# A vision tower's tokenizer: two linear layers folded into one product of 512 columns

## The chip, the core and the metric

The kernel runs on one core of one Trainium2 chip. The time is that of one execution on the device, in microseconds; the figure of the kernel before is the median of three runs. A core has a matrix engine (TensorE, PE in the profile, whose weight loads are listed as PEld), three more compute engines (VectorE or DVE, ScalarE or ACT, GpSimd or POOL) and SyncE (SP), which only issues transfers. Each engine works through its own queue of instructions in order; semaphores between them say when operands are ready. Products of TensorE go to PSUM, in which this kernel rotates seven tiles of 128 x 512 float32, called banks below.

## The reference

A tower of two transformer layers over four images of 3 x 224 x 224 in float32. Only the tokenizer is touched by the change. An image is cut into 28 x 28 patches of 8 x 8 x 3 = 192 numbers, 3136 tokens in all:

```python
tokens = layernorm(patches, ln1_g, ln1_b)
tokens = tokens @ W1 + b1                     # 192 -> 256
tokens = layernorm(tokens, ln2_g, ln2_b)
q = tokens
k = tokens
tokens = jnp.concatenate([q, k, tokens], axis=1)
h1 = layernorm(tokens @ Wp1 + bp1, lnp_g, lnp_b)   # 256 -> 256
h1 = jax.nn.silu(h1)
return h1 @ Wp2 + bp2                         # 256 -> 256
```

`layernorm` subtracts the mean over the features, multiplies by rsqrt(variance + 1e-5), then applies g and b. The concatenation makes three copies of each image's tokens, one after another; the shape of the later layers follows from it, but the kernel computes each token once. After the tokenizer come a layer with an attention across the images and routed experts (the token products with Wk, Wv and so on), and a layer with another attention and gated experts.

## The kernel before

**Tiles and groups.** Tokens are worked in 28 tiles of 112 (one tile is four rows of patches of one image, TT = 112), four tiles make a group (GT = 4), so there are seven groups. D = 256 is held in two chunks of 128 partitions where a token runs along the free axis, and 112 partitions where tokens are the partitions.

**Loads.** The image tile `img` holds one row of patches per partition (4 x 28 = 112), 24 rows of pixels (three colours by eight lines) and eight rows of zeros. It comes in four transfers, two on SP's and two on ScalarE's queue (L211). Behind them on SP are W1 (L219), Wp1, Wp2, the attention's weights, and then the zero fill of the two row buffers `xrows` and `yrows` that the experts use later (L253, 38 transfers of 1 MB). Behind them on ScalarE are the two rows of ln1. POOL's queue issues fifteen small constant loads (L170), then b1, bp1, bp2, bo (through `spread`, L184) and rb2, and then sets `nothing`, the source of the zero fill, to zero (L249). The norm rows ln2 and lnp are among the fifteen; one transposition (L446) makes columns of them.

**Patches.** A `manual_schedule` block (L430 to L448) fixes the order on TensorE and VectorE as written; elsewhere the tile scheduler decides it, and both engines keep their queue's order. For k = 0 to 6, `turn_patches(k)` (L338) turns four columns of patches: a half c takes 16 products with the identity (L347), each of which gives 32 rows for 112 patch rows. The rows lie in the 32-partition strip g, columns j of a half differ in their place along the free axis. ScalarE copies each half to `pT` (L352). Float32 products take two passes and are two records each. The order inside a half is

```python
for j in range(GT):
    for g in range(4):
        nc.tensor.matmul(pt[32 * g : 32 * (g + 1), j * TT : (j + 1) * TT], ...)
```

VectorE takes the statistics of the same pixels, one BN_STATS per column (L443). Ahead of k = 5 stands `first_layer()` (L356 to L395): it multiplies W1 by ln1_g, subtracts from each column its mean over the inputs (so the patch's own mean needs no subtraction), adds ln1_b W1 to b1, and permutes the rows of W1 to the order of `pT` (L390). After the last column `patch_scales` (L398 to L419) makes the reciprocals of all 3136 standard deviations (112 x 28) in one go and brings them to tokens as `rtok`.

**The loop.** `tokenize(g)` (L499 to L528) is a pipeline over three groups. In one call TensorE transposes the normalised rows of the second layer (group g-1) and of the third (group g-2), eight transposes each (L297), and then takes 16 passes for each of the three linear layers (L317): first layer of group g, second of g-1, third of g-2. ScalarE leaves the transposed rows with the norm's g and b applied (L492: Identity for ln2, Silu for lnp), and takes a square root per layer and group (L474). VectorE scales the first product by `rtok` and adds b1 (L466), or adds the bias of the later layers (L461), takes statistics and their aggregate per tile (L470, L471), the reciprocal (L479) and the normalised rows (L482). Calls 7 and 8, which finish the last groups, stand inside the first layer's attention (L1042, L1044), where the order of TensorE, VectorE and ScalarE is written out: `tokenize(7)`, keys and values of group 0, `tokenize(8)`, keys and values of group 1 and so on. Each of these starts with eight transposes of normalised tokens (L297).

## Time and profile before

| what | value |
|---|---|
| median of three runs | 854.3 us (852.16 to 854.61) |
| the profiled execution | 813.35 us |
| its span, first to last instruction | 811.6 us |
| mean granted TensorE clock | 0.973 |
| TensorE busy | 735.7 us, 91% |
| weight loads | 519.4 us, 64% |
| VectorE, ScalarE, POOL busy | 514.5, 318.5, 132.5 us |
| first turned patch on TensorE | 17.75 us |
| first product of the first layer | 40.18 us |
| start of the loop's passes (transposes) | 72.55, 85.06, 97.57, 110.09 us |
| transposes of the attention's groups 0 and 1 | 137.09, 151.17 us |

The profile is of one execution, which was shorter than the runs of the median; its durations and gaps belong together, and its own total is the 813.35. A line of the timeline gives start, duration, engine, source line, operation with its result and operands, the number of instructions gathered in it, and in brackets the idle time ahead of it with what ended it. A line of the windows gives, for a stretch of time, the busy time and number of instructions of PE, PEld, DVE, ACT and POOL, then the granted TensorE clock, the mean busy share of the 16 DMA engines and the rate in GB/s. In the slices of the span each digit is the busy share of a fortieth of the span (20.3 us) in tenths.

### The profile page before, as it was taken

The page shows a single profiled execution, that of the slowest core. Times are in us where ns is not written, and L with a number is a line of the kernel's source. Part 1 is how long each engine was busy: PE and PEld are TensorE (multiplying, and loading weights), DVE is VectorE, ACT ScalarE, POOL GpSimd, SP SyncE. Part 2 cuts the span into 40 slices and gives each one's busy share as a digit, 9 for nine tenths or more (in the row PEclk, how much of TensorE's full clock was granted, in tenths as well). Part 3 has the DMA queues.
Part 4 walks back from the last instruction along what each step waited for, and adds up shares of the span by engine and source line. Part 5 has one row for each costly group of instructions (what it writes and reads, how often), then busy time and mean ns, then how long its engine had stood idle before and what let it go on. Part 6 is the DMA issues. An engine that isn't in the chain of part 4 may idle for free. (4 is left out here: it accounts for less than half of the span.)

```text
span 811.6 us, 11184 instructions
## 1 busy us (share of the span) xinstructions
PE 735.7 (91%) x3669; PEld 519.4 (64%) x3669; DVE 514.5 (63%) x1619; ACT 318.5 (39%) x758; POOL 132.5 (16%) x151
## 2 busy tenths in 40 slices
PE   1879998899798887999999999799999999999996
PEld 1757785555455555887888887375776675555553
DVE  3477887576668886436445756699985655554431
ACT  0414443545375475443222322627544503222221
POOL 4200000000006360760012030775000000000000
PEclk9999999999999988999999999899999999999999
DMA  8999992000001168443334234232000002333323
GB/s 182 343 426 422 420 421 85 1 0 1 0 1 56 36 207 260 137 139 104 94 101 137 92 107 131 85 86 69 1 1 1 0 20 69 88 98 93 94 85 113
DMA packets 59182, 97.52 MB, mean 120 GB/s; under 512 B 15486, under 2 KB 49460, under 8 KB 54260
## 3 DMA queue, kind: packets, MB, share of 16 engines
q1 hardware_dynamic: 52700, 81.47, 29.1%
q0 software_dynamic: 6224, 14.13, 6.1%
q10 hardware_dynamic: 200, 1.21, 0.7%
q8 instruction: 29, 0.48, 0.2%
q14 instruction: 29, 0.24, 0.1%
HBM read 31.04 MB, written 65.74 MB: 119 GB/s over the span
## 5 line engine op out<-in xcount | busy, mean ns | idle before, releaser
L901 POOL DMA_INDIRECT xrows<-xn,pos x56 | 60.2, 1074 | 274.2 <-ACT kq L665 233.4
L1369 POOL DMA_INDIRECT ys<-yrows,pos x56 | 57.0, 1018 | 142.1 <-DMA yrows<-yb 126.0
L1173 PE MATMUL pb<-xTb,own 128*128 128x256 f32 x240 | 58.8, 389 | 3.8 <-DVE r L764 1.6
L1173 PE MATMUL pb<-hb,own 128*128 128x256 f32 x240 | 57.1, 380 | 0.3 <-DVE hb L1181 0.3
L1190 PE MATMUL pyb<-own,hb 128*128 128x256 f32 x240 | 57.0, 380 | 0.2 <-ACT hb L1179 0.2
L1179 ACT ACTIVATE hb<-pb,own 128x256 f32<-128x256 f32 x74 | 35.0, 473 | 55.9 <-PE pb L1173 47.5
L297 PE MATMUL pt<-ident,xn 112*128 112x112 f32 x280 | 42.2, 282 | 12.6 <-DVE xn L482 6.9
L1173 PEld LDWEIGHTS pb<-xTb,own 128*128 128x128 f32 x240 | 44.6, 194 | 12.5 <-ACT hb L1179 1.9
L1574 PE MATMUL pqk<-Wqkv,lxT 128*112 128x512 f32 x112 | 49.7, 594 | 0.5 <-ACT lxT L81 0.5
L1190 PEld LDWEIGHTS pyb<-own,hb 128*128 128x128 f32 x240 | 45.4, 190 | 6.7 <-ACT hb L1179 0.6
L297 PEld LDWEIGHTS pt<-ident,xn 112*128 112x128 f32 x280 | 32.4, 148 | 26.6 <-ACT xn L778 9.6
L1173 PEld LDWEIGHTS pb<-hb,own 128*128 128x128 f32 x240 | 43.3, 190 | 5.9 <-DVE hb L1181 0.9
L1196 DVE TENSOR_TENSOR yb<-pyb,eb 128x512 f32<-128x512 f32 x30 | 20.7, 690 | 39.2 <-PE pyb L1190 38.8
L306 PE MATMUL pe<-xT,eW 128*128 128x448 f32 x112 | 45.2, 546 | 0.0
L1163 ACT COPY xTb<-ptb 128x512 f32<-128x512 f32 x30 | 17.5, 583 | 64.3 <-PE ptb L1159 64.3
L1181 DVE TENSOR_SCALAR hb<-pb,own 128x256 f32<-128x256 f32 x46 | 22.1, 481 | 29.5 <-PE pb L1173 29.5
L317 PE MATMUL pwo<-Wo,oT 128*112 128x256 f32 x112 | 29.0, 413 | 7.5 <-DVE oT L730 6.7
L1574 PEld LDWEIGHTS pqk<-Wqkv,lxT 128*112 128x112 f32 x112 | 19.3, 177 | 24.8 <-issue 22.7
L690 DVE SCALAR_TENSOR_TENSOR prod<-kq 128x784 f32<-128x784 f32 x32 | 30.3, 968 | 7.3 <-ACT kq L665 5.1
L1582 ACT ACTIVATE qk<-qk 112x256 f32<-112x256 f32 x56 | 22.8, 407 | 27.9 <-DVE qk L1578 25.4
L306 PEld LDWEIGHTS pe<-xT,eW 128*128 128x128 f32 x112 | 20.2, 190 | 20.9 <-issue 20.7
L1150 DVE COPY own<-ew 128x1540 f32 x30 | 28.9, 963 | 5.0 <-issue 1.5
(339 smaller groups left out, 1520.1 us busy)
## 6 DMA issues: line engine op xcount, KB each, us to landing
xrows<-nothing SPq DMA_DIRECT2D x19, 1024.0 KB
yrows<-nothing SPq DMA_DIRECT2D x19, 1024.0 KB
out_dram<-h SPq DMA_DIRECT2D x84, 112.0 KB
xb<-xrows SPq DMA_DIRECT2D x30, 256.0 KB
yrows<-yb SPq DMA_DIRECT2D x30, 256.0 KB
ew<-in_L_ffn_expert_w_dram SPq DMA_DIRECT2D x6, 768.0 KB
wb<-wd SPq DMA_DIRECT2D x28, 112.0 KB
img<-in_x_dram ACTq DMA_DIRECT2D x2, 588.0 KB
```

What stands on the lines that cost most here:

```text
L297: nc.tensor.transpose(pt[:, j * TT : (j + 1) * TT], xn[:, j, c * P : (c + 1) * P], ident[:TT, :TT])
L306: nc.tensor.matmul(pm[: wcols.stop - wcols.start, :n], w[:, c, wcols], xT(c), start=(c == 0), stop=(c == chunks - 1),)
L317: nc.tensor.matmul(pm[:, i, :], xT(c, t), w[:, c, :], start=(c == 0), stop=(c == chunks - 1))
L690: nc.vector.scalar_tensor_tensor(prod, qTs[s][:, o, :], 1.0, kT[:, o, t * SEQ : (t + 1) * SEQ], ALU.mult, ALU.mult, accum_out=atts[s][:, o ...
L901: put = nc.gpsimd.indirect_dma_start(out=xrows[:, :], out_offset=bass.IndirectOffsetOnAxis(ap=pos[:, k, t0 + j : t0 + j + 1], axis=0), in_ ...
L1150: nc.vector.tensor_copy(w, ewf[0][:, bass.ds(off, EW)])
L1173: nc.tensor.matmul(pm, wm[:, c, o * P : (o + 1) * P], src[:, c, :], start=(c == 0), stop=(c == 1),)
L1179: nc.scalar.activation(dst[:, o, :], pm, AF.Relu, bias=b)
L1190: nc.tensor.matmul(pm[:, t, :], src[:, c, t * P : (t + 1) * P], wm[:, c, :], start=(c == 0), stop=(c == 1),)
L1369: got = nc.gpsimd.indirect_dma_start(out=y[:, j, k, :], out_offset=None, in_=yrows[:, :], in_offset=bass.IndirectOffsetOnAxis(ap=pos[:, k, ...
L1574: nc.tensor.matmul(pqk, xT[:, c, cut(j, 1)], Wqkv[:, c, : 2 * D], start=(c == 0), stop=(c == 1),)
L1582: nc.scalar.activation(half, half, AF.Square, accum_out=ss[:, j, i : i + 1])
```

## The change

Because W1 has had its column means taken out, a token after the first layer is p/s with p = x W1c + s b1', where x are the raw pixels, s is the patch's standard deviation (the root of variance + eps) and b1' = b1 + ln1_b W1. The second norm of p/s is (p - mean p) / sqrt(var p + eps s²), so s only enters under the root. The second layer is linear in that, so its weights are folded in: `Wall` holds, side by side, W1c with the row b1' (256 columns, of which only the variance of p is used) and that matrix times W2 (256 columns), where W2 is ln2_g Wp1 with its column means taken out. The std is written into the image tile's zero row 24, one number per patch, and is turned with the pixels; it meets b1' in the product.

So `first_layers` (once, ahead of all patches) makes `Wall`; `patch_stds(k)` makes the standard deviations of four columns ahead of their `turn_patches(k)`; in `turn_patches` the strip g is now the outer and the column j the inner loop; `scaled_variances` brings eps s² to tokens as `ev`; `first_rows(g)` takes the product of 512 columns, one tile to a PSUM bank, of which ScalarE copies the right half and VectorE takes the statistics of the left, and then makes the rows of the third layer. The rows between the first and the second layer are no longer normalised or transposed. The second layer's product, its `y2`, and the Identity with ln2 are gone. Loads of ln1, ln2, W1 and Wp1 now stand ahead of the image on ScalarE's and SP's queues, and b1 and bp1 are issued next on POOL's. The diff, cut:

```diff
-    allones = const.tile([TT, TT], F32, tag="allones", name="allones")
+    allones = const.tile([P, P], F32, tag="allones", name="allones")
...
-        ("ln2_g", "L0_tok_ln2_g"), ("ln2_b", "L0_tok_ln2_b"), ("lnp_g", "L0_tok_lnp_g"),
-        ("lnp_b", "L0_tok_lnp_b"), ("gamma", "L0_attn_gamma"), ("beta", "L0_attn_beta"),
+        ("lnp_g", "L0_tok_lnp_g"), ("lnp_b", "L0_tok_lnp_b"), ("gamma", "L0_attn_gamma"), ("beta", "L0_attn_beta"),
...
     img = tokp.tile([TT, 32, WID], F32, tag="img", name="img")
+    ln1 = tokp.tile([2, PD], F32, tag="ln1", name="ln1")
+    nc.scalar.dma_start(out=ln1[:1], in_=a["L0_tok_ln1_g"].unsqueeze(0))
+    nc.scalar.dma_start(out=ln1[1:], in_=a["L0_tok_ln1_b"].unsqueeze(0))
+    ln2 = tokp.tile([4, P], F32, tag="ln2", name="ln2")
+    nc.scalar.dma_start(out=ln2[:2], in_=a["L0_tok_ln2_g"].rearrange("(r p) -> r p", p=P))
+    nc.scalar.dma_start(out=ln2[2:], in_=a["L0_tok_ln2_b"].rearrange("(r p) -> r p", p=P))
+    W1 = tokp.tile([KP, 2, D], F32, tag="W1", name="W1")
+    nc.sync.dma_start(out=W1, in_=a["L0_tok_W1"].rearrange("(s p) n -> p s n", p=KP))
+    Wp1 = tokp.tile([P, 2, D], F32, tag="Wp1", name="Wp1")
+    nc.sync.dma_start(out=Wp1, in_=a["L0_tok_Wp1"].rearrange("(c p) n -> p c n", p=P))
     for b in range(NI):
 ...
-    ln1 = tokp.tile([2, PD], F32, tag="ln1", name="ln1")
-    nc.scalar.dma_start(out=ln1[:1], in_=a["L0_tok_ln1_g"].unsqueeze(0))
-    nc.scalar.dma_start(out=ln1[1:], in_=a["L0_tok_ln1_b"].unsqueeze(0))
-    W1 = tokp.tile([KP, 2, D], F32, tag="W1", name="W1")
-    nc.sync.dma_start(out=W1, in_=a["L0_tok_W1"].rearrange("(s p) n -> p s n", p=KP))
+    b1 = spread(tokp, "b1", a["L0_tok_b1"])
+    bp1 = spread(tokp, "bp1", a["L0_tok_bp1"])
     nc.vector.memset(img[:, CY:, :], 0.0)
...
-    b1 = spread(tokp, "b1", a["L0_tok_b1"])
-    Wp1 = tokw.tile([P, 2, D], F32, tag="Wp1", name="Wp1", bufs=1)
-    nc.sync.dma_start(out=Wp1, in_=a["L0_tok_Wp1"].rearrange("(c p) n -> p c n", p=P))
-    bp1 = tokw.tile([TT, D], F32, tag="bp1", name="bp1", bufs=1)
-    nc.gpsimd.dma_start(out=bp1, in_=a["L0_tok_bp1"].partition_broadcast(TT))
     Wp2 = tokw.tile([P, 2, D], F32, tag="Wp2", name="Wp2", bufs=1)
     nc.sync.dma_start(out=Wp2, in_=a["L0_tok_Wp2"].rearrange("(c p) n -> p c n", p=P))
...
+    SROW = 3 * 32 + CY
     def turn_patches(k):
         for c in range(2):
             pt = ps_tile("ptp")
-            for j in range(GT):
-                for g in range(4):
+            for g in range(4):
+                for j in range(GT):
                     nc.tensor.matmul(
                         pt[32 * g : 32 * (g + 1), j * TT : (j + 1) * TT],
                         img[:, :, (k * GT + j) * PATCH + 4 * c + g], ident[:TT, :TT],
...
+    def without_mean(w, n, dim):
+
+        pm = ps_tile("pmean")[:n, :D]
+        for i in range(2):
+            nc.tensor.matmul(pm, allones[:n, :n], w[:, i, :], start=(i == 0), stop=(i == 1))
+        for i in range(2):
+            nc.vector.scalar_tensor_tensor(
+                w[:, i, :], pm, -1.0 / dim, w[:, i, :], ALU.mult, ALU.add
+            )
-    def first_layer():
...
+    def first_layers():
+        gb = tokp.tile([P, 8], F32, tag="gbT", name="gbT")
...
+        nc.tensor.transpose(pt[:, 4:8], ln2, ident[:4, :4])
+        nc.vector.tensor_copy(gb[:KP, :4], pt[:KP, :4])
+        nc.vector.tensor_copy(gb[:, 4:], pt[:, 4:8])
...
         W1g = tokp.tile([KP, 2, D], F32, tag="W1g", name="W1g")
+        W2 = tokp.tile([P, 2, D], F32, tag="W2", name="W2")
         for i in range(2):
+            nc.vector.tensor_scalar(W1g[:, i, :], W1[:, i, :], g1(i), None, ALU.mult)
+        for i in range(2):
+            nc.vector.tensor_copy(
+                bb[:KP, i, :], gb[:KP, 2 * i + 1 : 2 * i + 2].to_broadcast([KP, TT])
+            )
+        without_mean(W1g, KP, PD)
         pw = ps_tile("pbw")[:TT, :D]
         for i in range(2):
+            nc.tensor.matmul(pw, bb[:KP, i, :], W1[:, i, :], start=(i == 0), stop=(i == 1))
         nc.vector.tensor_tensor(b1, pw, b1, ALU.add)
         pp = ps_tile("pwc").rearrange("p (i d) -> p i d", i=2)
         for i in range(2):
             for half in range(2):
                 nc.tensor.matmul(
                     pp[:, i, :], perm[:, half, i].rearrange("p g k -> p (g k)"),
+                    W1g[:, half, :], start=(half == 0), stop=(half == 1 and i == 0),
+                )
+        nc.tensor.matmul(pp[:, 1, :], srow, b1[:1, :], start=False, stop=True)
+        Wall = tokp.tile([P, 2, 2 * D], F32, tag="Wall", name="Wall")
+        nc.vector.tensor_copy(Wall[:, :, :D], pp)
+        for c in range(2):
+            nc.vector.tensor_scalar(W2[:, c, :], Wp1[:, c, :], g2(c), None, ALU.mult)
+        for c in range(2):
...
+        without_mean(W2, P, D)
+        WcT = tokp.tile([P, 2, 2 * P], F32, tag="WcT", name="WcT")
+        pt = ps_tile("pwct").rearrange("p (f k) -> p f k", f=2)
+        for f in range(2):
+            for i in range(2):
+                nc.tensor.transpose(
+                    pt[:, f, i * P : (i + 1) * P], Wall[:, i, f * P : (f + 1) * P], ident
+                )
+        nc.scalar.copy(WcT, pt)
+        pw = ps_tile("pbw2")[:TT, :D]
+        for c in range(2):
+            nc.tensor.matmul(pw, bb[:, 2 + c, :], Wp1[:, c, :], start=(c == 0), stop=(c == 1))
+        nc.vector.tensor_tensor(bp1, pw, bp1, ALU.add)
+        pp = ps_tile("pw2").rearrange("p (i d) -> p i d", i=2)
+        for i in range(2):
+            for f in range(2):
+                nc.tensor.matmul(
+                    pp[:, i, :], WcT[:, f, i * P : (i + 1) * P], W2[:, f, :],
+                    start=(f == 0), stop=(f == 1),
+                )
+        nc.vector.tensor_copy(Wall[:, :, D:], pp)
+        return Wall
+    def patch_stds(k):
+        w0 = k * GT
+        for w in range(w0, w0 + GT):
+            nc.vector.bn_stats(pst[:, w, :], img[:, :CY, w * PATCH : (w + 1) * PATCH])
+        st, v = pst[:, w0 : w0 + GT], pv[:, w0 : w0 + GT]
+        d = tokp.tile([TT, GT], F32, tag="pd", name="pd")
         nc.vector.tensor_tensor(d, st[:, :, 1], st[:, :, 4], ALU.subtract)
         nc.vector.tensor_tensor(v, st[:, :, 2], st[:, :, 5], ALU.add)
         nc.vector.scalar_tensor_tensor(d, d, PD / 4.0, d, ALU.mult, ALU.mult)
         nc.vector.tensor_tensor(v, v, d, ALU.add)
-        nc.scalar.activation(v, v, AF.Sqrt, bias=eps[:TT], scale=1.0 / PD)
-        nc.vector.reciprocal(v, v)
+        nc.scalar.activation(
+            img[:, CY, w0 * PATCH : (w0 + GT) * PATCH].rearrange("q (w x) -> q w x", x=PATCH)[
+                :, :, PATCH - 1
+            ],
+            v, AF.Sqrt, bias=eps[:TT], scale=1.0 / PD,
+        )
+    def scaled_variances():
+        nc.vector.tensor_scalar(pv, pv, 1e-5 / PD, 1e-10, ALU.mult, ALU.add)
...
-        rtok = tokp.tile([TT, NT], F32, tag="rtok", name="rtok")
-        nc.vector.tensor_copy(rtok, pr)
-        return rtok
+        ev = tokp.tile([TT, NT], F32, tag="ev", name="ev")
+        nc.vector.tensor_copy(ev, pr)
+        return ev
...
+    srow = tokp.tile([1, P], F32, tag="srow", name="srow")
     pst = tokp.tile([TT, HP, 6], F32, tag="pst", name="pst")
+    pv = tokp.tile([TT, HP], F32, tag="pv", name="pv")
     with tc.manual_schedule(engines={mybir.EngineType.DVE, mybir.EngineType.PE}):
...
+        Wall = first_layers()
         for k in range(HP // GT):
-            if k == 5:
-                W1g = first_layer()
+            patch_stds(k)
             turn_patches(k)
-            for w in range(k * GT, (k + 1) * GT):
-                nc.vector.bn_stats(pst[:, w, :], img[:, :CY, w * PATCH : (w + 1) * PATCH])
-        rtok = patch_scales(pst)
+        ev = scaled_variances()
...
-    def added(pm_of, dst, bias, stats, scale=None):
...
+    def first_rows(g):
+        t0 = groups[g][0]
+        y = tokp.tile([TT, GT, D], F32, tag="y", name="y", bufs=2)
+        st = small.tile([TT, GT, 6], F32, tag="st", name="st")
+        mv = small.tile([TT, GT, 2], F32, tag="mv", name="mv")
+        for j in range(GT):
+            pm = ps_tile("pw1")[:TT]
+            for c in range(2):
+                nc.tensor.matmul(
+                    pm, pTf[:, c, cut(t0 + j, 1)], Wall[:, c, :], start=(c == 0), stop=(c == 1)
+                )
+            nc.scalar.copy(y[:, j, :], pm[:, D:])
+            nc.vector.bn_stats(st[:, j, :], pm[:, :D])
+            nc.vector.bn_aggr(mv[:, j, :], st[:, j, :])
+        r = small.tile([TT, GT], F32, tag="rstd", name="rstd")
+        nc.vector.tensor_tensor(r, mv[:, :, 1], ev[:, t0 : t0 + GT], ALU.add)
+        nc.scalar.activation(r, r, AF.Sqrt, bias=zero[:TT])
+        nc.vector.reciprocal(r, r)
+        st = small.tile([TT, GT, 6], F32, tag="st", name="st")
+        mv = small.tile([TT, GT, 2], F32, tag="mv", name="mv")
+        for j in range(GT):
+            nc.vector.scalar_tensor_tensor(
+                y[:, j, :], y[:, j, :], r[:, j : j + 1], bp1, ALU.mult, ALU.add
+            )
+            nc.vector.bn_stats(st[:, j, :], y[:, j, :])
+            nc.vector.bn_aggr(mv[:, j, :], st[:, j, :])
+        r = small.tile([TT, GT], F32, tag="rstd", name="rstd")
+        nc.scalar.activation(r, mv[:, :, 1], AF.Sqrt, bias=eps[:TT])
         nc.vector.reciprocal(r, r)
         xn = tokw.tile([TT, GT, D], F32, tag="xn", name="xn")
         for j in range(GT):
             )
         return xn
-    def turned_rows(xn, func, g, b):
-        xT = tokw.tile([P, 2, GN], F32, tag=f"xT{g}", name=f"xT{g}")
+    def turned_rows(xn):
+        xT = tokw.tile([P, 2, GN], F32, tag="xTt", name="xTt")
         def put(c, pt):
-            nc.scalar.activation(xT[:, c, :], pt, func, scale=col(g, c), bias=col(b, c))
+            nc.scalar.activation(
+                xT[:, c, :], pt, AF.Silu, scale=col("lnp_g", c), bias=col("lnp_b", c)
+            )
         transposed(xn, GT, put)
         return xT
-    second, third = {}, {}
+    normed, third = {}, {}
     def tokenize(g):
+        if g < len(groups):
+            normed[g] = first_rows(g)
         if 1 <= g <= len(groups):
-            tT = turned_rows(second.pop(g - 1), AF.Identity, "ln2_g", "ln2_b")
+            third[g - 1] = turned_rows(normed.pop(g - 1))
         if g >= 2:
-            sT = turned_rows(third.pop(g - 2), AF.Silu, "lnp_g", "lnp_b")
-        if g < len(groups):
...
-        if g >= 2:
+            sT = third.pop(g - 2)
             t2 = groups[g - 2][0]
-            added(
-                lambda two: mm_rows(two, lambda c, j: sT[:, c, cut(j, 1)], Wp2, "pwp2"),
-                h[:, t2 : t2 + GT, :], bp2, False,
-            )
-        if 1 <= g <= len(groups):
-            third[g - 1] = rows_of(y2, stats2)
+            for two in halves(range(GT)):
+                nc.vector.tensor_tensor(
+                    h[:, t2 + two[0] : t2 + two[0] + 2, :],
+                    mm_rows(two, lambda c, j: sT[:, c, cut(j, 1)], Wp2, "pwp2"),
+                    over(bp2, 2), ALU.add,
+                )
```

## The prediction

> **What bounds the kernel now.** I read the page's busy shares and slices, then the timeline of the first 160 us, since the change touches nothing later, and last the windows of one loop pass.
>
> ```profile
> PE 735.7 (91%) x3669; PEld 519.4 (64%) x3669; DVE 514.5 (63%) x1619; ACT 318.5 (39%) x758; POOL 132.5 (16%) x151
> PE   1879998899798887999999999799999999999996
> ```
>
> TensorE is busy 91% of the span; the one empty stretch is the first slice (20 us), and no later stage is tied to an absolute time: the zero fill of the two row buffers, the only long transfer, has all but landed at 126 us, and nothing waits for it before 137.7. A shift of the tokenizer therefore reaches the end whole. From the timeline, the start of it:
>
> ```profile
> 17.75 8.07 PE L347 MATMUL ptp<-ident,img 112*32 112x112 f32 x218 [14.79 <-DMA img<-in_x_dram]
> 20.59 0.57 POOL L184 DMA_DIRECT2D b<-in_L_tok_b_dram  x1
> 24.39 0.54 ACT L352 COPY pT<-ptp 128x448 f32<-128x448 f32 x1 [0.21 <-PE ptp L347]
> 25.16 0.54 ACT L352 COPY pT<-ptp 128x448 f32<-128x448 f32 x1 [0.23 <-PE ptp L347]
> 26.10 2.73 PE L347 MATMUL ptp<-ident,img 112*32 112x112 f32 x102 [0.28 <-issue]
> 32.12 1.97 PE L390 MATMUL pwc<-W1g,perm 96*128 96x256 f32 x8 [0.61 <-DVE W1g L383]
> 36.93 0.22 DVE L402 TENSOR_TENSOR pd<-pst 112x28 f32<-112x28 f32 x1
> 40.18 5.31 PE L317 MATMUL pw<-Wc,pT 128*112 128x256 f32 x16
> ```
>
> The reader sees: patches are turned as soon as the image lands (17.7); bias b1 is only issued at 20.6 and its tile's row says 5.3 us to landing; the weights are prepared in the middle (28.8 to 34.8); the std arithmetic is done once, for all 28 columns (36.9); the first product starts at 40.2. Half a group of patches (32 rows of L347) takes 25.16-24.39 = 0.77 us. And one steady pass of the loop:
>
> ```profile
> 85.06 0.93 PE L297 MATMUL pt<-ident,xn 112*128 112x112 f32 x8
> 86.58 0.60 PE L317 MATMUL pw<-Wc,pT 128*112 128x256 f32 x2
> 87.64 3.19 PE L317 MATMUL pw<-Wc,pT 128*112 128x256 f32 x14
> 90.67 3.62 PE L317 MATMUL pwp<-Wp,xTln_g 128*112 128x256 f32 x16
> 94.12 3.62 PE L317 MATMUL pwp<-Wp,xTlnp_g 128*112 128x256 f32 x16
> 85.06:97.57 12.51, 12.17 (x65) 9.98 (x64) 10.57 (x35) 5.84 (x8) 0.00 (x0) 1.00 1.01 420
> ```
>
> A pass is 12.51 us and TensorE's: three linear layers of 3.45 (start to start), two sets of eight transposes at 0.89, waits 0.38. VectorE has 10.57 of work, ScalarE 5.84.
>
> [...] a pass of 256 columns takes 3.45/16 = 0.216 us, so 112 columns should take 0.094; 102 in 2.73 us is 0.027, so about 3.5 run at once. [...] Here:
>
> ```profile
> 217.43 7.55 PE L317 MATMUL pwo<-Wo,oT 128*112 128x256 f32 x26 [3.47 <-DVE oT L730]
> 249.65 5.87 PE L317 MATMUL pwo<-Wo,oT 128*112 128x256 f32 x26 [1.39 <-DVE oT L730]
> ```
>
> 1.7 us lost after a wait of 3.47; I take 1.9 for each such gap (at 40.18: 5.31 against 3.45). [...] the trace has 1.28 and no drain (load at 60.64, ACTIVATE at 61.93). [...]
>
> **The change, part by part.**
>
> *Weights first.* first_layers stands ahead of the patches on TensorE and VectorE, both in written order. It needs b1 (added, then multiplied in as a row through srow). b1's issue on POOL comes two loads earlier (2 x 0.52) but behind an image that lands up to 1 us later (448 KB of weights now go ahead of it): landing 25.5 against 25.9. All patches queue behind it. From 25.5: add 0.4, row product 0.7, copy to Wall 0.7, scaling and broadcast of the second weight 0.9 with its mean product (1.0 and more) beside it, two subtractions 0.75, bias product 1.0, folded product 2.0 (as L390): patches start on TensorE at about 32.6 instead of 17.75, VectorE reaches its statistics at 33.3. The waits cost nothing only for VectorE and ScalarE, which have nothing else; for TensorE it is 15 us of work not done.
>
> *Statistics and std per four columns.* 28 BN_STATS at 0.265 and 28 small operations (four in 0.67): 7 x (1.06+0.71) = 12.4 on VectorE, plus seven square roots (0.3) hidden beside copies. Alone this would end at 45.7 and give a first product at about 47.3.
>
> *The loop over strips.* turn_patches now has the strip g outside and the column j inside, so eight passes in a row (four columns, two passes each, 448 rows for 224 products) go to one strip. Whether they still overlap [...] no row of before shows it. Bounds: [...] 0.77 a half as now, and VectorE's 12.4 decides; or [...] 7 x 0.094 = 0.66 per strip, 2.64 a half, 37 us for 14. [...] 5 x 0.094 = 0.47; a half is 4 x 0.47 = 1.87, fourteen are 26.2, and 1.9 for the cold clock: patches end at 32.6+28.1 = 60.7, copy and small products 0.9, first product 61.6, against 40.2.
>
> *Loop.* The second layer's eight products per pass go, the first has 512 columns: 16 passes at 0.43 (L1574's twelve take 5.15), 6.9 us, the same columns as before. Gone are eight transposes (0.89), the 0.38 wait, two ACTIVATEs of 0.67. TensorE: 6.9+0.89+3.45 = 11.25. VectorE: statistics 8 x 0.37, aggregates 8 x 0.15, scaling 4 x 0.42, normalising 1.37, output adds 1.37, small 0.7: 9.3. ScalarE: four copies of 256 columns (bound 0.25 to 0.45, taken 0.4), two roots 0.6, Silu 1.34, but four table loads 5.1: 8.6. So TensorE stays the bound if the chain fits. Walk it from the end P of a pass's last product: output add 0.9 (latency included), reciprocal 0.1, scaling and second statistics 4.2 to P+5.2; ScalarE meanwhile Silu to P+1.9, copy of the second tile at P+3.9, table load to 5.2, root 5.6; two statistics and aggregates, reciprocal P+6.1, normalised rows P+6.45 to 7.5. TensorE's four tiles end at P+6.9: the first transposes find their rows, the last are 0.1 to 0.2 late. Pass 11.4, no slack.
>
> *Edits taken at nothing, and their cover.* Seven loads change place on SP's and ScalarE's queues: W1 and Wp1 now ahead of two image loads on SP, four norm rows ahead of two on ScalarE (issues of 0.3 to 0.6 each). One image load on each queue also waits for an earlier small load to land, and Wp2 and the attention weights are queued behind SP's; the cover is that b1 lands some 7 us after the image in any case, and Wp2 is first needed past 70 us. Without that cover a late image would shift all patches one for one. bp1 lands 0.5 after b1, 5 us before its add. POOL's zeroing, behind both, starts within 1 us of where it did, so the fill ends near 126 and its wait (the first mT) is met at 140. Four rows fewer in the constants' transposition, the larger all-ones tile and the root instead of a root and a reciprocal are below 0.3 together.
>
> *Sum from the first product to the second attention group's transposes.* Before: 151.17-40.18 = 111.0. After: two groups' products 13.8, wait for the first rows 0.7 and transposes 0.9, third group 6.9, wait 0.25, transposes and third layer 4.3: 26.8; four passes 45.6; the last group has no product to hide its chain: VectorE also takes four statistics of h first, rows complete at 8.0, transposes 8.3, third layer 3.45 on a cold clock +1.9: 13.6; then transposes, keys and values, third layer of the last group, 11.1 (14.1 before, with a wait of 1.89 that goes). Total 97.1, a gain of 13.9.
>
> Net on the profiled execution: +21.4-13.9 = +7.5; with 0.5 for small waits +8 on its 813.35. The median of the runs, 854.3, stands 5.0% above the profiled execution, which I read as the same work at a slower pace: +8.4, so **863**.
>
> **The rivals.**
> [...] Then the first product is at 47.3, +7.1-13.9 = -6.8: 847. [...] It decides at a half of 1.4 us: 14 x 1.4 is 7 us above the 12.4 that VectorE sets.
> *No look ahead:* 37+1.9, first product 72.4, +18.3: 873.
> *Wide look ahead, but the chain sets the pass.* ScalarE's four loads and the two roots per pass add 1.2 (each copy or statistic 0.15 longer would do): five passes take back 6, leaving about 854. For it: no slack in the walk; against it: VectorE and ScalarE both have 2 us free per pass.
>
> **How the numbers follow.** Forecast 0.42 (857 to 869 by itself), no look ahead 0.15, wide look ahead 0.35, wide with chain 0.08. 0.3% is 2.6 us, about what a measurement of this kernel can tell from no change. Faster is the third case but for 0.02: 0.33; same 0.08; slower 0.59. The range runs from the third case less 2 (845) to the second plus 3 (876).
>
> **What would show it.** First row of the new product near 61.6 (47 if the strips overlap, 72 if not), halves of 1.9, 0.8 or 2.6 us between pT copies; patches starting at 32 to 33 right behind the folded product; b1's landing at 25 to 26; 11.4 between passes; a TensorE gap of about 7 us before the last group's transposes. It is wrong if b1 lands after 29, if the passes take over 12.3, or if the halves are below 1.4.

## The result

The changed kernel takes 858.45 us (median of four runs, 857.94 to 858.95) against 853.23 (four runs, 850.70 to 854.61): a ratio of 1.0065 with a 95% interval of 1.0037 to 1.0092, slower by 5 us. The forecast was 863, with a range from 845 to 876. In the table further down, one run of "pairs of columns" and three of "b1 early, columns outside" are left out of the medians and ratios as slow runs, over 1.5% above the fastest of their kernel.

The profiled execution of before that the prediction worked on (813.35) was an exception: no other run of this kernel took less than 846. A second profile of the same kernel spans 852.0, and the profile after 857.2; these two can be compared to the end, and the first only up to the attention.

### The profile page after: what moved, and what is told of

Its sections match the earlier page's. It is cut to its first block, busy times and chain, and to the rows that moved or that the text cites. A ratio compares the mean times of both kernels' runs of the same rounds, so it can differ in the third digit from the quotient of the medians.

```text
span 857.2 us, 10929 instructions
## 1 busy us (share of the span) xinstructions
PE 756.6 (88%) x3524; PEld 518.7 (61%) x3524; DVE 504.4 (59%) x1620; ACT 334.0 (39%) x789; POOL 129.1 (15%) x149
## 5 line engine op out<-in xcount | busy, mean ns | idle before, releaser
L1415 POOL DMA_INDIRECT ys<-yrows,pos x56 | 55.0, 981 | 164.3 <-DMA yrows<-yb 134.0
L1236 PE MATMUL pyb<-own,hb 128*128 128x256 f32 x240 | 59.6, 392 | 4.4 <-ACT hb L1225 4.4
L517 PE MATMUL pw<-Wall,pT 128*112 128x512 f32 x112 | 49.3, 593 | 0.0
L1242 DVE TENSOR_TENSOR yb<-pyb,eb 128x512 f32<-128x512 f32 x30 | 20.7, 691 | 45.1 <-PE pyb L1236 34.5
L298 PE MATMUL pt<-ident,xn 112*128 112x112 f32 x224 | 34.7, 287 | 12.4 <-DVE xn L540 6.8
L1694 PE MATMUL pukx<-xa,uk 112*128 112x258 f32 x112 | 29.0, 416 | 18.1 <-ACT uk L1652 18.1
L298 PEld LDWEIGHTS pt<-ident,xn 112*128 112x128 f32 x224 | 27.1, 152 | 26.8 <-issue 8.7
L1694 PEld LDWEIGHTS pukx<-xa,uk 112*128 112x128 f32 x112 | 22.7, 209 | 21.9 <-issue 18.4
L517 PEld LDWEIGHTS pw<-Wall,pT 128*112 128x112 f32 x112 | 19.6, 177 | 25.1 <-issue 21.4
```

The costliest lines, as they stand in the source:

```text
L298: nc.tensor.transpose(pt[:, j * TT : (j + 1) * TT], xn[:, j, c * P : (c + 1) * P], ident[:TT, :TT])
L517: nc.tensor.matmul(pm, pTf[:, c, cut(t0 + j, 1)], Wall[:, c, :], start=(c == 0), stop=(c == 1))
L1236: nc.tensor.matmul(pm[:, t, :], src[:, c, t * P : (t + 1) * P], wm[:, c, :], start=(c == 0), stop=(c == 1),)
L1415: got = nc.gpsimd.indirect_dma_start(out=y[:, j, k, :], out_offset=None, in_=yrows[:, :], in_offset=bass.IndirectOffsetOnAxis(ap=pos[:, k, ...
L1694: nc.tensor.matmul(pg, uks[u][:, k, c * P : (c + 1) * P], xas[u % 4][:, k, : D + 2], start=(j == 0), stop=(j == TPI - 1),)
```

## The profile after

First the page of the changed kernel, engines and slices of 21.4 us:

```profile
PE 756.6 (88%) x3524; PEld 518.7 (61%) x3524; DVE 504.4 (59%) x1620; ACT 334.0 (39%) x789; POOL 129.1 (15%) x149
PE   3699996999789878799999999348999999999996
```

TensorE makes 145 passes fewer than before (3524 for 3669) and is still the busiest engine. Slices 26 to 28 (3, 4, 8) are a stop that the first profile of before lacks; it is dealt with below. The start of the span, in the timeline:

```profile
26.11 0.42 DVE L400 TENSOR_TENSOR b<-pbw,b 112x256 f32<-112x256 f32 x1 [13.79 <-DMA b<-in_L_tok_b_dram]
26.59 1.22 PE L408 MATMUL pwc<-b,srow 1*128 1x256 f32 x2 [10.67 <-DVE b L400]
34.52 3.62 PE L354 MATMUL ptp<-ident,img 112*32 112x112 f32 x56
39.06 22.12 PE L354 MATMUL ptp<-ident,img 112*32 112x112 f32 x392 [0.92 <-ACT img L452]
40.08 0.53 ACT L359 COPY pT<-ptp 128x448 f32<-128x448 f32 x1 [1.07 <-PE ptp L354]
41.84 0.53 ACT L359 COPY pT<-ptp 128x448 f32<-128x448 f32 x1 [1.23 <-PE ptp L354]
61.61 13.99 PE L517 MATMUL pw<-Wall,pT 128*112 128x512 f32 x32
138.91 2.08 PE L298 MATMUL pt<-ident,xn 112*128 112x112 f32 x8 [6.82 <-DVE xn L540]
```

The bias b1 is added at 26.1 and patches start at 34.5. A half of four columns takes 1.76 us (41.84-40.08), the first product of 512 columns is at 61.6, and ahead of the last group's transposes TensorE waits 6.8. One pass of the loop, in the windows (PE, PEld, DVE, ACT, POOL busy, clock, DMA share, GB/s):

```profile
94.41:105.51 11.10, 11.10 (x42) 6.36 (x40) 8.21 (x31) 8.45 (x12) 0.00 (x0) 1.00 1.01 421
```

A pass is 11.10 where it was 12.51, and TensorE doesn't wait in it at all. The second attention group's transposes come at 157.18.

**Where the two profiles of before differ.** Lines of the second profile of before (first three), and of after:

```profile
39.25 3.71 PE L317 MATMUL pw<-Wc,pT 128*112 128x256 f32 x16
148.64 0.93 PE L297 MATMUL pt<-ident,xn 112*128 112x112 f32 x8
564.04 6.65 PE L1648 MATMUL pukx<-xa,uk 112*128 112x258 f32 x16 [18.38 <-ACT uk L1606]
```

```profile
568.99 6.60 PE L1694 MATMUL pukx<-xa,uk 112*128 112x258 f32 x16 [18.06 <-ACT uk L1652]
```

The stop of 18 us at the start of the second layer is there with and without the change. From the second layer's first product to its first output product, 36.0 us pass in the first profile of before (503.7 to 539.7), 61.0 in the second (519.0 to 580.0), 60.5 after (524.4 to 584.9). The experts took 189.7 in the first profile, 207.3 in the second, 204.5 after (from their first transposes on, 314.1, 311.7 and 320.0). So the 40 us belong to that one execution. In the tokenizer the second profile is even ahead of the first, 148.64 against 151.17: 0.9 of this is an earlier first product, and 1.6 is that the first products took 3.71 us where those of the first profile, which began at a granted clock of 0.50 (40.18 to 42.00), took 5.31. The change therefore delays the second attention group by 6.0 to 8.5 us, and the runs show 3 to 8 (the interval on 853).

## The experiments

The table has two marks from each profile: the first product of the first layer and the second attention group's transposes. Ratios are to the kernel before, measured beside each. From the second group to the end of the span, every profile but the first of before takes 696 to 707 us (before 703.4, changed 700.0). A shift of the tokenizer thus reaches the end, but one execution shows it only to within some 5 us.

| kernel | median us | ratio, 95% interval | first product | second group |
|---|---|---|---|---|
| before (second profile) | 853.71 (one run) | | 39.25 | 148.64 |
| changed | 858.45 | 1.0065 [1.0037, 1.0092] | 61.61 | 157.18 |
| columns outside | 860.55 | 1.0092 [1.0054, 1.0129] | 57.98 | 153.97 |
| pairs of columns | 857.78 | 1.0075 [1.0038, 1.0112] | 55.13 | 151.11 |
| before, strips outside | 863.69 | 1.0138 [1.0096, 1.0179] | 52.64 | 161.95 |
| columns outside, fill late | 869.57 (one run) | | 48.19 | 164.06 |
| b1 early | 845.92 | 0.9921 [0.9880, 0.9963] | 48.55 | 144.29 |
| b1 early, columns outside | 843.86 | 0.9899 [0.9861, 0.9938] | 46.18 | 142.31 |
| weights at k = 5, columns outside | 851.31 | 0.9982 [0.9954, 1.0009] | 50.24 | 144.91 |
| b1 early, columns outside, fill late from its own pool | 832.19 | 0.9764 [0.9702, 0.9825] | 37.44 | 132.62 |
| the same, keys and values first | 835.06 | 0.9793 [0.9741, 0.9846] | 37.03 | 134.17 |
| b1 early, strips outside, fill late from its own pool | 845.07 | 0.9921 [0.9895, 0.9947] | 47.92 | 143.22 |
| before, fill late from its own pool | 850.47 | 1.0001 [0.9971, 1.0030] | 39.86 | 150.62 |

**Before once more**, without an edit.

> The kernel before once more, for a second profile of it. The profile after is 6.0 us behind the profile before at the second attention group's transposes (157.18 against 151.17), but 45.6 us behind at the end: 14.7 more come in the experts' phase, 24 more at the end of it. My theory: these 39 us belong to the execution and not to the change, and the runs of the kernel before (851 to 855) have them too; then this profile has a span near 850, a long wait of TensorE for ScalarE around the end of the experts' phase, and the same 151 at the second attention group. The rival: the change causes them, through the later start or the different addresses of its tiles; then this profile ends near 812 again.

Span 852.0, the same stop of 18 us as after the change, second group at 148.64 (151 was expected): the first reading holds, and the prediction's way of taking the median for the same work at a slower pace does not.

**Before with the strips outside.**

```diff
-            for j in range(GT):
-                for g in range(4):
+            for g in range(4):
+                for j in range(GT):
```

> The kernel before with the strip g outside and the column j inside, nothing else changed. Strip theory: its halves go from 0.77 to 1.76 us, 14 of them add 12 to 14 us ahead of the first product (52 to 54 instead of 40.2), and the run is about 13 us longer than before: 866, 1.5% slower. Std rival: there is no std in the image tile here, so halves stay at 0.77 and the time does not change.

In its timeline:

```profile
17.54 20.59 PE L347 MATMUL ptp<-ident,img 112*32 112x112 f32 x320 [14.57 <-DMA img<-in_x_dram]
24.10 0.53 ACT L352 COPY pT<-ptp 128x448 f32<-128x448 f32 x1 [2.03 <-PE ptp L347]
25.86 0.53 ACT L352 COPY pT<-ptp 128x448 f32<-128x448 f32 x1 [1.23 <-PE ptp L347]
```

Halves of 1.76, the first product 13.4 later than in the second profile of before (52.64-39.25), the second group 13.3 later, the run 11 to 12 longer. The order of the strips alone makes the patches slow here; there is no std.

**The change with the columns outside**, and **with pairs of columns**.

```diff
-            for g in range(4):
-                for j in range(GT):
+            for j in range(GT):
+                for g in range(4):
```

```diff
-            for g in range(4):
-                for j in range(GT):
+            for j, g in [(j, g) for two in halves(range(GT)) for g in range(4) for j in two]:
+                if True:
```

> The changed kernel with the column j outside and the strip g inside again in turn_patches. Strip theory ([...] eight passes in a row to one strip run one after the other): halves go from 1.76 us to 0.82, where VectorE's 1.64 for four columns sets the pace; first product at 48 instead of 61.6, about 13.4 us less than the changed kernel, 845, some 1% faster than before. Rival (the patches are paced by the std that ScalarE writes into the image tile, behind its copies): halves stay at 1.76 and the time stays at 858.

> The changed kernel with two columns in a row to one strip, then the next strip, then the other two columns: runs of four passes instead of eight. Strip theory [...] the runs overlap nearly in full, halves 0.8 to 0.9 us, time as with the columns outside, 845. Rival within it (passes to the same strip lose in proportion, whatever the length of the run; 4.7 of 8 passes serial now): 2.35 of 4, eight runs a half, halves stay at 1.76, 858. Std rival: 858.

In both texts the strip theory is that eight passes in a row to one strip make the halves of 1.76; how TensorE goes on behind such a pass no trace shows, only the time of a half is measured. The theory's time of 845 failed in both kernels. The rivals' time of 858 came out, but not their reason for it, halves that stay at 1.76. Three copies of the patches in the kernel with pairs, and one of its stops:

```profile
42.81 0.54 ACT L359 COPY pT<-ptp 128x448 f32<-128x448 f32 x1
43.58 0.54 ACT L359 COPY pT<-ptp 128x448 f32<-128x448 f32 x1 [0.23 <-PE ptp L354]
44.34 0.54 ACT L359 COPY pT<-ptp 128x448 f32<-128x448 f32 x1
47.45 5.09 PE L354 MATMUL ptp<-ident,img 112*32 112x112 f32 x128 [2.16 <-issue]
```

Here halves take 0.77 with runs of four passes to a strip, as those in the prediction's lines of before with runs of two; with a loss in proportion to the run they would have stayed at 1.76. But the patches as a whole gain much less than the 13 us that were expected: from the first patch to the first product it takes 27.1 us after the change, 24.8 with the columns outside and 21.4 with the pairs. TensorE's timeline of the columns outside shows why:

```profile
36.45 5.18 PE L354 MATMUL ptp<-ident,img 112*32 112x112 f32 x136 [2.07 <-ACT img L452]
43.27 3.31 PE L354 MATMUL ptp<-ident,img 112*32 112x112 f32 x128 [1.65 <-issue]
50.02 4.92 PE L354 MATMUL ptp<-ident,img 112*32 112x112 f32 x128 [3.43 <-issue]
56.76 0.79 PE L354 MATMUL ptp<-ident,img 112*32 112x112 f32 x18 [1.82 <-issue]
```

There are three stops that no engine ends ("issue"), and exactly 128 passes between them. 128 passes with their weight loads (x128 each in the timeline) are 256 instructions. The stops come after 174, 302 and 430 of the 448 passes (38 stand ahead of these lines). The pairs stop after 302 and 430 as well, so the place belongs to the instruction and not to the order of the strips. The DMA view of the same kernel from 33 to 57 us (share of the engines in 40 slices; then queue, packets, MB and share):

```profile
DMA  9999999999999999999999999999999999999999
...
q1 hardware_dynamic: 1385, 10.07, 100.3%
q8 instruction: 3, 0.05, 0.7%
```

The engines are full with the zero fill, and three packets of 16 KB come through on the instruction queue, 7 us apart: they start in the microseconds from 40, 47 and 54, and TensorE goes on two to three microseconds after each. This gave the fetch theory: the stops go with these packets, one packet to 256 instructions, a packet per 7 us while the fill runs, against the 3.1 us (four halves of 0.77) that TensorE takes for 128 passes.

The profiled second group came 3.2 (columns) and 6.1 us (pairs) sooner than after the change, but the medians are hardly better than 858.45. In the profiled executions part of the gain or all of it is lost behind the tokenizer: from the second group to the end 705.1 and 702.5 us pass, against 700.0 after the change. The runs scatter more, too (855.93 to 865.62 and 854.04 to 864.90, against 857.94 to 858.95, of four runs only). Stops that differ in length between executions could add to this; what the scatter comes from was not shown.

**The fill held back**, to test the fetch theory: its source is set to zero by VectorE behind the patches.

```diff
-    nc.gpsimd.memset(nothing, 0.0)
-    for r in range(0, XROWS, 8 * P):
...
         nc.vector.tensor_copy(cols, pc[:, :nrows])
+        nc.vector.memset(nothing, 0.0)
+        for r in range(0, XROWS, 8 * P):
...
```

> The changed kernel with the columns outside, and the zero fill of the row buffers held back until the patches are turned (its source is zeroed by VectorE behind them). With the columns outside TensorE stood still three times for 1.6 to 3.4 us with no other engine as the releaser, and each time went on after 128 records, when a packet of 16 KB on the instruction queue had landed; 448 records took 24.8 us. Fetch theory: [...] without it the patches take 12 to 13 us at VectorE's pace of 1.64 per four columns, first product at 46 to 48, no such gaps; the fill then ends near 150 and the first attention products wait for it. Rival: the pauses are in TensorE or come from the order of the strips; then they stay, first product 55 to 58.

Lines of its timeline:

```profile
35.57 12.20 PE L345 MATMUL ptp<-ident,img 112*32 112x112 f32 x410 [2.09 <-ACT img L443]
48.19 13.99 PE L516 MATMUL pw<-Wall,pT 128*112 128x512 f32 x32
152.30 1.34 ACT L1066 ACTIVATE mT<-pt,cols 128x448 f32<-128x448 f32 x2 [22.52 <-DMA yrows<-nothing]
```

410 passes go in one piece, the stops are gone, and the first product is 9.8 us sooner than with the fill running (0.9 of it is an earlier start of the patches). So these stops came with the fill, and with its packets 7 us apart. That TensorE lacks instructions in them is read from the count of 128 and the packets; no record of the trace names the cause. The run also shows the price of this place for the fill: ScalarE stands still for 22.5 us ahead of the attention's first tokens, until the fill ends at 152, because they lie where its source lay (with a source in a pool of its own, below, this wait is gone).

**b1 early**, **b1 early with columns outside**, and **the weights at k = 5**.

```diff
-    b1 = spread(tokp, "b1", a["L0_tok_b1"])
-    bp1 = spread(tokp, "bp1", a["L0_tok_bp1"])
+    b1 = spread(tokp, "b1", a["L0_tok_b1"], eng=nc.scalar)
+    bp1 = spread(tokp, "bp1", a["L0_tok_bp1"], eng=nc.scalar)
     for b in range(NI):
```

```diff
-        Wall = first_layers()
         for k in range(HP // GT):
+            if k == 5:
+                Wall = first_layers()
```

> The changed kernel with b1 and bp1 loaded on ScalarE's queue ahead of the image instead of on POOL's behind fifteen loads; strips outside as in the change. Wait theory: the 10.7 us that TensorE waits for b1 (13.0 to 26.6) go, the rest of the weight chain is 8 us, so patches start at 23 to 25 instead of 34.5; halves stay at 1.76, first product at 51, 10 us less than the changed kernel: 848. Rival: the image, which lands at 18, or the instruction supply is next, and the gain is below 5 us: 854 or more.

> b1 and bp1 early and the columns outside. Fetch theory: the patches start at 24, run at full rate for about 170 records and starve from the start of the zero fill (26) on, 128 records per 6.7 us; first product at 47 to 50, hardly before that of the strips with b1 early (51), 845 to 848. Rival (the pauses have another cause and are independent of the fill): full rate, first product at 38, 836.

> The fold without the two changes of order: columns outside, and the weights prepared at k = 5 as in the kernel before, everything else as in the change (std per four columns, product of 512 columns). Most patches are turned before the fill starts and before b1 lands: k = 0 to 4 from 17.5 to 27, weights 27 to 35, the rest to 39 or, if the supply of instructions fails, 42; first product at 41 to 44 against 39 to 40 of the kernel before. From there to the second attention group 95.6 us as after the change, against 109.4 to 111: about 11 us faster than before, 842, 1.3%. Rival (the gain of the loop depends on the late start, for example because the fill's end at 126 holds the attention back when it comes sooner): 850 or more.

The first two in TensorE's timeline, b1 early and then with the columns outside as well:

```profile
21.49 3.59 PE L354 MATMUL ptp<-ident,img 112*32 112x112 f32 x56
48.55 13.99 PE L517 MATMUL pw<-Wall,pT 128*112 128x512 f32 x32
```

```profile
37.67 6.04 PE L354 MATMUL ptp<-ident,img 112*32 112x112 f32 x128 [3.98 <-issue]
44.97 0.79 PE L354 MATMUL ptp<-ident,img 112*32 112x112 f32 x18 [1.26 <-issue]
46.18 15.68 PE L517 MATMUL pw<-Wall,pT 128*112 128x512 f32 x32
```

The wait for b1 is worth 13 us, where 10 were expected: with b1 early the patches start at 21.5 and both marks are 13 sooner, with halves of 1.76 as in the change; the median is 12.5 lower. With the columns outside as well the first product is at 46.18, not 38: TensorE stops for 3.98 and 1.26 us, again after 302 and 430 passes, and packets on the instruction queue start in the microseconds from 35 and 42, two to three before each restart, as the fetch theory had it. The order of the strips is worth little as long as the fill runs (first product at 46.18 against 48.55, the run 843.86 against 845.92).

The kernel with the weights at k = 5 missed its first mark (41 to 44) and its time (842). Its timeline:

```profile
19.92 8.46 PE L354 MATMUL ptp<-ident,img 112*32 112x112 f32 x218 [16.96 <-DMA img<-in_x_dram]
32.00 0.25 PE L380 MATMUL pgb<-ident,ln 2*96 2x2 f32 x2
44.20 1.23 PE L354 MATMUL ptp<-ident,img 112*32 112x112 f32 x38
50.24 13.99 PE L518 MATMUL pw<-Wall,pT 128*112 128x512 f32 x32
```

The image lands 2.2 to 2.8 us later behind the moved weights (17.12 to 17.75 in the kernels of before), and the weights take 12.2 us of TensorE's time in the middle of the patches (32.0 to 44.2), where I had expected 8 and the single layer of before took about 5. From the first product to the second group it takes 94.7, as after the change (95.6), so the gain of the loop does not hang on the late start. What the loop gains is spent ahead of it: 0.2% faster, which can't be told from no change.

**The fill late, from a pool of its own.** Four kernels, with this edit beside the ones shown above:

```diff
-    nothing = tokp.tile([P, 8 * D], F32, tag="nothing", name="nothing")
+    nothing = tokw.tile([P, 8 * D], F32, tag="nothing", name="nothing", bufs=1)
```

and in the one with keys and values first:

```diff
-        tokenize(len(groups))
         keys_values(0)
+        tokenize(len(groups))
```

> The changed kernel with four things: columns outside, b1 and bp1 early, the zero fill held back until the patches are turned, and the fill's source in a pool that is not freed before the attention, so that the attention's normalised tokens do not wait for the fill. Fetch theory: patches at full supply from 22, first product at 37 to 38 (15.9 after the first patch, as with the fill held back), second attention group's transposes 96 later at 133 to 134, 8 to 9 before those of the kernel with b1 early and columns outside (142.3); the run 837, 1.8% faster than before. Rival: the patches starve without the fill too, or the fill, now from 40 to 140, takes its time from something else in the loop; then the first product is at 44 or later, or the passes are above 11.3, and the run stays at 846.

> The kernel with b1 early and the fill held back in a pool of its own, but with the strips outside as in the change: against the kernel with the columns outside (first product 37.4, second attention group 132.6, run 832) it tells what the order of the loop costs when the supply of instructions is no limit. Strip theory: halves of 1.76 as with the fill running, patches 22 to 48, first product at 48, second attention group at 144, the run 843. Rival (it is the fill that set the 1.76, by way of the supply of instructions, 128 records in 6.7 to 7.0 us): halves below 1, first product at 38, 833.

> The kernel before with the zero fill held back until its patches are turned, from a source in a pool of its own. It tells whether the gain of the last version is one that the kernel before could have had as well. Fetch theory: its patches are turned before the fill begins or at a full supply (0.77 us a half both before and after the start of the fill), so it gains nothing: first product at 39 to 41, the run 853. Rival: the fill costs the kernel before as much as the changed one, and the run is at 845 or less.

> As the kernel with the fill held back in a pool of its own, and in the attention the keys and values of group 0 stand ahead of the tokenizer's last transposes. In the changed kernel TensorE waits 6.8 us there for the rows of the last group (VectorE's chain), and the keys and values of group 0 (6.3 us of products) need nothing of it. Theory: they fill the wait; the second attention group's transposes come 6 us sooner (127 to 128) and the run is at 831, 2.5% faster than before. Rival: the attention's own chain (statistics of h, ScalarE's normalised tokens, whose tables alternate) is late as well and only 2 to 3 us are gained: 834.

First products of the kernel with the columns outside, of the one with the strips outside (behind two of its copies), and of the kernel before:

```profile
37.44 13.99 PE L516 MATMUL pw<-Wall,pT 128*112 128x512 f32 x32
```

```profile
36.98 0.53 ACT L350 COPY pT<-ptp 128x448 f32<-128x448 f32 x1 [1.03 <-PE ptp L345]
38.74 0.53 ACT L350 COPY pT<-ptp 128x448 f32<-128x448 f32 x1 [1.02 <-PE ptp L345]
47.92 13.99 PE L516 MATMUL pw<-Wall,pT 128*112 128x512 f32 x32
```

```profile
39.86 5.16 PE L308 MATMUL pw<-Wc,pT 128*112 128x256 f32 x16
```

Now the order of the strips costs its 10.5 us and the runs follow, 832 against 845. The halves with the strips outside are 1.76 again, without any fill; and in the change, with the same 1.76, the granted clock was 1.00 from 32.1 to 61.6. So 1.76 is neither the fill's nor the clock's. The kernel before gains nothing from the late fill (850.47, ratio 1.0001), so the 832 comes from the change with the late fill, the early bias and the columns outside together. It is the fastest version, 2.4% below before (1.8 to 3.0).

Keys and values first gained nothing; the second group came 1.6 us later, and the runs (835) can't be told from 832. The rival rightly had the attention's own chain late as well, but it is so late that the wait grew:

```profile
116.40 1.38 DVE L1056 TENSOR_SCALAR xn<-h,mv,rstd 112x256 f32<-112x256 f32 x4
116.96 2.07 PE L289 MATMUL pt<-ident,xn 112*128 112x112 f32 x8 [9.45 <-DVE xn L1056]
```

VectorE makes the attention's rows behind the last tokens' rows (113.8 to 115.1), so these are the later of the two, and TensorE waits 9.45 us instead of 6.82. To close the gap it is VectorE's order that would have to change; this wasn't tried.

## Why the prediction was right, step by step

- *First product at 61.6:* measured 61.61, and that it fits so well is luck, since two errors of 1.9 cancel. The patches start at 34.5 instead of 32.6. Of this, 0.6 is b1, which was issued at 21.12 (20.59 before), not two loads earlier. The other 1.3 is the chain from b1 to the patches, 8.4 instead of 7.1. Its row product took 1.22 instead of 0.7: behind the wait of 10.67 TensorE's granted clock was 0.50 from 26.6 to 32.1 (with b1 early, without that wait, the same product takes 0.69). From the first patch to the first product it took 27.1 instead of 29.0: halves of 1.76 instead of 1.87 make 1.5 of it. The 1.9 that the prediction takes for a cold clock (5.31 against 3.45 at 40.18, granted clock 0.50 there) were put here, where the clock was 1.00; a wait of 0.92 for ScalarE's first std came instead.
- *Halves of 1.87:* 1.76, and the order of the strips as the cause is right, shown by the strips alone in the kernel before. The step to the number was the author's estimate: of the eight passes to a strip five one after the other, at 0.094 each. A strip takes 1.76/4 = 0.44, or 4.7 passes of that estimated 0.094. "Wide look ahead" in the prediction is the rival on the other side, "no look ahead" a half of 2.64; no row of before decides between the three, their weights (0.42, 0.35, 0.15) were the author's estimate, and what TensorE does with a pass that waits no trace shows. The measured times tell this much: a pass follows another to its strip 24 times in a half of the pairs (eight runs of four) and 28 times in one with the strips outside (four runs of eight), nearly as often, and the halves take 0.77 and 1.76 us. It is the length of the runs that costs, not the number of passes behind one to the same strip.
- *b1 is waited for:* right, 10.7 us of TensorE's time, and 12.5 us of the run by the kernel with b1 early.
- *The pass:* 11.10 for 11.4. TensorE's sum of 11.25 was nearly right; the small waits that I added for the chain did not come, VectorE having 8.21 of work instead of 9.3. ScalarE, with four table loads a pass of 1.28 us each (the load at 60.64 in the prediction is one of before), has 8.45 (8.6 expected) and sets nothing.
- *First product to the second attention group:* 95.6 for 97.1, with the wait of 6.8 for about 7 that was forecast. Before: 111.0 in the first profile and 109.4 in the second, of which the 1.6 of the first products (5.31 against 3.71) is the difference. The gain is 13.8 to 15.4 (13.9 forecast).
- *From the profile to the median:* wrong. The prediction took the median's 5% above the profiled execution for the same work at a slower pace and scaled 8 us to 8.4. The extra 40 us were two stretches elsewhere, and the tokenizer had no part in them; nothing was to be scaled. It cost little here: the scaling and the 0.5 added for small waits are 0.9 of the forecast shift of 8.7 (863 - 854.3). At the second group the shift is 6.0 against the profile that the prediction worked on, for which it had 7.5, and 8.5 against the second profile. The runs show 5.2, with 3 to 8 in the interval. The range of 845 to 876 holds the rivals' times (847, 854 and 873) with the forecast, so the time alone could not have told them apart; the marks do.
- *The rival on the other side* (the strips overlap, first product at 47.3, 847): its sum came near only without the stops. With the columns outside the first product was at 57.98, and at 48.19 once the fill was out of the way. The step that failed in it is the rate of 0.77 a half, carried from before to patches that lie wholly in the fill. In before 218 of the 448 passes come ahead of the fill (it begins at 25.7), and the weights, with few instructions in 5.2 us, stand between the others. The line at 26.10 in the prediction, 0.28 us with "issue" after 218 passes, looks like a small stop of the same kind: a packet on the instruction queue starts 2.5 to 2.8 us before it ends. The forecast, too, had no such stops in it, and it is luck that this cost nothing: the strips take 4 x 1.76 = 7.0 us for 128 passes, and from 48 us on the packets in the change start 7 apart (in the microseconds from 48, 55 and 62), and no stop is seen there.

## What to carry to other kernels

When many short instructions are moved to another time, look at what the DMA engines do then: with them full, TensorE got through 128 passes with their loads in 6.5 to 7.3 us here (restart to restart) instead of 3.1, and stops with "issue" as the releaser, 128 passes apart, were the sign of it. Where the order of products to the 32-partition strips is free, try short runs to one strip: four passes in a row cost nothing here (0.77 us a half, as with two), eight more than doubled the time (1.76). And ahead of scaling a profile to a median, take a second profile: a gap may sit in one place that the change doesn't touch.

## What the runs showed of the hardware that was not expected

- Beside a zero fill at 422 GB/s, packets of 16 KB on the instruction queue started 7 us apart (columns outside), and TensorE stopped for 1.65, 3.43 and 1.82 us, 128 passes between the stops. Without the fill, in the fastest version, the packets started 3 to 4 us apart (in the microseconds from 26, 29, 33 and 37), and one stop of 0.47 us was left.
- After the stop of 3.43 us TensorE's 128 passes took 4.92 instead of 3.31. With the pairs they took 5.09 after a stop of 2.16, and with b1 early and the columns outside 6.04 after one of 3.98; after the 1.65 with the columns outside they took 3.31. What slowed them was not shown.
- A half of the patches took 0.77 us at best with runs of two passes to one 32-partition strip (before, columns outside) or of four (pairs). With runs of eight it took 1.76, with a std (the change) and without (before, strips outside), beside the fill and without it.
